# Column attention and feed-forward of a two-layer convolution and attention kernel: three column groups in work at a time, and the output tile written by ScalarE

## The chip, the cores and the metric

The kernel runs on one core of one Trainium2 chip. The metric is the time of one execution in microseconds (us), measured on the device. Five engines work side by side, each through its own queue in order: PE (TensorE, matrix products and transposes into PSUM; PEld are its weight loads), DVE (VectorE), ACT (ScalarE), POOL (GpSimd, here mostly an issuer of stores) and SP (SyncE, which issues loads).

## The reference, cut to what matters

The input is (4, 64, 256, 256) in fp32. Two layers follow each other; only the end of the second one is touched. With `h` as (batch, row, column, 64 channels) that end computes

```
hc = _ln(h.swapaxes(1, 2), cn_g, cn_b)
h = h + _lin_attn(hc, col_wq, ..., col_bo).swapaxes(1, 2)
f = _ln(h, fn_g, fn_b)
f = gelu(f @ w1.T + b1, approximate=False) @ w2.T + b2
return jnp.moveaxis(h + f, -1, 1)
```

`_ln` is a layer norm over the channels. `_lin_attn` runs along a column, over its 256 rows, with 4 heads and one value of q and k per head: q and k become elu + 1, k is divided by its sum and q by its mean over the rows, `ktv` is the sum over the rows of k times v (16 channels per head), and the output is q times `ktv`, times `wo`, plus a bias. The feed-forward goes from 64 channels to 256 and back.

## The kernel before, in words

The kernel runs in stages, one after another; intermediate results lie in HBM. The last stage, `stage_d` (L1124 to L1334), reads `hd`, the result of the row attention, and writes the output. Its unit is a *column group*: one image and 32 of its columns, with all 256 rows. There are 4 x 8 = 32 groups. A group's tile `h` has 128 partitions (rows of one half of the image) x 32 columns x 2 halves x 64 channels, 16 KB per partition, and is loaded by four DMAs on SP (L1157).

For each group there are two Python generators, which trace instructions up to a `yield` and then let the other trace:

- `attn` does the attention of the group and prepares the feed-forward. For each of eight steps `r` of 4 columns: every second step `spread` (L1160 to L1169) takes 8 columns: sum over channels (L1163, DVE), difference from the mean `xc` (L1165, DVE), its square (L1167, ACT), sum of squares (L1168, DVE). The columns are transposed (L1188, PE), copied from PSUM (`xT`, L1190, ACT) and multiplied with the weights of q and k (L1197, PE). After four steps the scores are turned back (L1201, DVE). Then comes `rstd` (L1173 a square root on ACT, L1175 a reciprocal on DVE), the scaling and bias (L1204, L1205), the exponential (`feature`, L680 and L681) and the features `f` and `kz` (L1214, L1217). With these follow the sums over the rows (L1223, L1227, L1230), the reduction to `zn` (L1234 to L1241), its transpose (L1244, L1246), the 4-head map (`mix`, L687 to L695, and L1250), and the result, added to `h` in place (L1256 and L1259 on PE, L1262 on DVE), once for each half of the rows. At last comes the norm for the feed-forward: `spread` again, `rstd`, and the normed tile `xf` of 8 columns (L1273, DVE).
- `ffn` does the feed-forward in eight turns of 4 columns: transpose of `xf` (L1283), copy `xfT` (L1285, ACT), four hidden tiles of 128x512 (L1296, PE), each with its gelu (`hg`, L1298, ACT), then the transpose of `h` into PSUM (L1304) and on top of it the second product (L1307), and the sum plus bias written to the output tile `st` (L1309, DVE). `st` holds two groups (64 columns), is written in the order row, column, so with a stride of 256 bytes, and goes to HBM with eight DMAs on POOL (L1332) after every second group.

The driver pairs `attn` of group n with `ffn` of group n-1 (`_steps`, L239: one `yield` of each in turn). So an iteration begins with the transposes of the normed tiles that the end of the iteration before has made. `h` has three buffers, `xf` five, most other tiles of the stage two or one; PSUM is shared by six tiles `mm` and two `sm`, each 128x512. The written order is a priority: the framework places instructions on each engine's queue at build time by its own estimate of when each is ready, so that the order on an engine can differ from the written one. An activation function outside of the loaded set costs ScalarE a table load (ACT_TABLE_LOAD in the trace); in this stage gelu, square root and exponential change the set.

Of the kernel before, what the change touches and what calls it, by code (L numbers as in the profile page):

```python
# [9 lines left out]
F32 = mybir.dt.float32  # L10
# [237 lines left out]
def kernel(ctx: ExitStack, tc: tile.TileContext, x, packs, fd, out, off):  # L248
# [875 lines left out]
    def stage_d():  # L1124
        with ExitStack() as cs:
# [27 lines left out]
            def load(b, g):  # L1153
                h = p.tile([128, 32, 2, C], F32, name="h", bufs=3)
                for rh in (0, 1):
                    for j in (0, 1):
                        SY.dma_start(h[:, 16 * j:16 * j + 16, rh, :], hd[b, rh * 128:(rh + 1) * 128, :, 2 * g + j, :])  # L1157
                return h

            def spread(src, n, s2):  # L1160

                s1 = p.tile([128, n], F32, tag="ln_s", name="ln_s")
                V.tensor_reduce(s1, src, AX.X, ALU.add)  # L1163
                xc = p.tile([128, n, C], F32, tag="xc", name="xc")
                V.scalar_tensor_tensor(xc, bc(s1, C), -LN_S, src, ALU.mult, ALU.add)  # L1165
                sq = p.tile([128, n, C], F32, tag="ln_sq", name="ln_sq")
                S.activation(sq, xc, AF.Square)  # L1167
                V.tensor_reduce(s2, sq, AX.X, ALU.add)  # L1168
                return xc  # L1169

            def rstd(s2, n):
                s3 = p.tile([128, n], F32, tag="ln_d", name="ln_d")
                S.activation(s3, s2, AF.Sqrt, bias=eps_t, scale=LN_S)  # L1173
                s4 = p.tile([128, n], F32, tag="ln_r", name="ln_r")
                V.reciprocal(s4, s3)  # L1175
                return s4

            def attn(h, xfs):

                qp = p1.tile([128, 32, 32], F32, name="qp")  # L1180
                v1 = p1.tile([128, 64], F32, name="v1")
                for r in range(8):
                    if r % 2 == 0:
                        k = r // 2
                        spread(h[:, 8 * k:8 * k + 8].rearrange("p c a e -> p (c a) e"), 16, v1[:, 16 * k:16 * k + 16])
# [5 lines left out]
                    yield  # L1191
                    if r % 4 == 0:
                        qk = sm()
# [5 lines left out]
                    if r % 4 == 3:  # L1199

                        V.transpose(qp[:, r // 4 * 16:r // 4 * 16 + 16].rearrange("p c m -> p (c m)"), qk)  # L1201
# [4 lines left out]
                yield  # L1206
# [8 lines left out]
                fv = f.rearrange("p r k c h -> p r k (c h)")  # L1215
                kz = p1.tile([128, 2, 128], F32, name="kz")
                V.tensor_tensor(kz.rearrange("p r (c h) -> p r c h", h=4), f[:, :, 1], rs.rearrange("p (c r) -> p r c", r=2).unsqueeze(3).to_broadcast([128, 2, 32, 4]), ALU.mult)  # L1217
                yield

                t = mm()  # L1220
                for rh in (0, 1):
                    for g in range(4):
                        T.matmul(t[g * 32:(g + 1) * 32, :], kz[:, rh, g * 32:(g + 1) * 32], h[:, 8 * g:8 * g + 8, rh, :], start=(rh == 0), stop=(rh == 1))  # L1223
                qs = sm()
# [39 lines left out]
                for hf in (0, 1):  # L1264
                    v2 = p.tile([128, 32], F32, name="v2")
                    xcs = []
                    for k in (2 * hf, 2 * hf + 1):
                        xcs.append(spread(h[:, 8 * k:8 * k + 8].rearrange("p c a e -> p (c a) e"), 16, v2[:, (k % 2) * 16:(k % 2) * 16 + 16]))
                        yield
                    rs = rstd(v2, 32)  # L1270
                    for k in (0, 1):
                        xf = p.tile([128, 8, 2, C], F32, name="xf", bufs=5)
                        V.tensor_tensor(xf.rearrange("p c a e -> p (c a) e"), xcs[k], bc(rs[:, k * 16:k * 16 + 16], C), ALU.mult)  # L1273
                        xfs.append(xf)

            def ffn(h, xfs, st, gi):


                def first(r):
                    t = mm()  # L1280
                    xf = xfs[r // 2]
                    for i in range(4):
                        T.transpose(t[:, i * 128:(i + 1) * 128], xf[:, (r % 2) * 4 + i].rearrange("p a e -> p (a e)"), ident)  # L1283
                    xT = p.tile([128, 512], F32, name="xfT")
                    S.copy(xT, t)  # L1285
                    return xT

                yield
                xT = first(0)
                for r in range(8):  # L1290
                    yield
                    hg = []
                    for i in (0, 1):
                        for rh in (0, 1):
                            t = mm()
                            T.matmul(t, w1[rh * 64:(rh + 1) * 64, i * 128:(i + 1) * 128], xT[rh * 64:(rh + 1) * 64], start=True, stop=True)  # L1296
                            g = p.tile([128, 512], F32, tag=f"hg{rh}{i}", name=f"hg{rh}{i}")
                            S.activation(g, t, AF.Gelu, bias=b1[:, i:i + 1])  # L1298
                            hg.append(g)
                    nx = first(r + 1) if r < 7 else None  # L1300
                    yield
                    y = mm()
                    for i in range(4):
                        T.matmul(y[:, i * 128:(i + 1) * 128], h[:, r * 4 + i].rearrange("p a e -> p (a e)"), ident, is_transpose=True, start=(i == 0), stop=False, skip_group_check=True)  # L1304
                    for i in (0, 1):
                        for rh in (0, 1):
                            T.matmul(y[rh * 64:(rh + 1) * 64, :], w2[:, i, :], hg[i * 2 + rh], start=False, stop=(i == 1), skip_group_check=True)  # L1307
                    c = gi * 32 + r * 4
                    V.tensor_scalar(st[:, :, c:c + 4].rearrange("p r c -> p c r"), y.rearrange("p (c r) -> p c r", c=4), K("b2"), None, ALU.add)  # L1309
                    xT = nx  # L1310

            seq = [(b, g) for b in range(B) for g in range(8)]
            hs = {0: load(*seq[0])}
            xfs = {}
            st = None
            for n in range(len(seq) + 1):
                if n + 1 < len(seq):
                    hs[n + 1] = load(*seq[n + 1])
                xfs[n] = []
                ga = attn(hs[n], xfs[n]) if n < len(seq) else None  # L1320
                gf = None
                if n >= 1:
                    b, g = seq[n - 1]
                    if g % 2 == 0:
                        st = p.tile([128, 128, 64], F32, name="st")
                    gf = ffn(hs.pop(n - 1), xfs.pop(n - 1), st, g % 2)
                _steps(ga, gf)
                if n >= 1 and g % 2 == 1:
                    for i in range(4):
                        for rh in (0, 1):  # L1330
                            r = rh * 128 + i * 32
                            G.dma_start(out[b, :, r:r + 32, g // 2 * 64:g // 2 * 64 + 64], st[rh * 64:(rh + 1) * 64, i * 32:(i + 1) * 32])  # L1332
# [22 lines left out]
```

## Time and profile before

| | |
|---|---|
| three runs | 9063.34 us median (9060.01 to 9071.98) |
| the profiled execution | 9063.4 us, span of the trace 9061.6 us |
| busy in the span | PE 8382.1 us (93%), DVE 5945.5 (66%), ACT 4740.4 (52%), POOL 1135.0 (13%) |
| first product of the last stage to its last | 6812.9 to 9033.2 us |
| last output DMA issued | 9042.3 us |
| the stage between the first and the last of the feed-forwards | 6870.5 to 8989.1 us: PE busy 1887.0, DVE 1690.6, ACT 1467.5 |

A row of the profile's groups reads: line, engine, operation, output tile <- input tiles, shape, number of instructions, then busy us in total, mean ns of one, and the engine's idle time just before them with what ended it. The chain of waits follows the work that ended last, back through whatever released each step; its lines are start, length and what. A line of the list of waits reads: who waited, for whom, us in total, times, longest. Busy PE isn't PE at its peak, since matmuls are pipelined. A fp32 product appears as two instructions, so that the four hidden tiles of a turn are eight L1296.

### The profile page before, as it was taken

How to read it: one execution, taken by the hardware profiler on the slowest of the kernel's cores; microseconds unless marked ns; L12 is line 12 of the kernel's file. 1: busy time of each engine (PE TensorE's matmuls, PEld its weight loads, DVE VectorE, ACT ScalarE, POOL GpSimd, SP SyncE). 2: the span in 40 equal slices, each digit the busy share in tenths (PEclk: the TensorE clock that was granted, in tenths of full speed). 3: DMA queues.
4: the chain of work that ended last, by engine and by line, in shares of the span. 5: the costliest groups of instructions: out<-in, count | busy, mean ns of one | idle time of the engine just before them, and what ended most of it. 6: DMA issues, size and time to landing. Idle time of an engine off the chain costs nothing. (4 is left out here: it accounts for less than half of the span.)

```text
span 9061.6 us, 136047 instructions
## 1 busy us (share of the span) xinstructions
PE 8382.1 (93%) x53934; PEld 4354.5 (48%) x53934; DVE 5945.5 (66%) x8509; ACT 4740.4 (52%) x7844; POOL 1135.0 (13%) x1828
## 2 busy tenths in 40 slices
PE   8999999789999998999999999999997888898897
PEld 7877777534444443333333344444453333333333
DVE  6666666467777775222222288888887778878876
ACT  4455555545555554222222266666655767766765
POOL 1111111112221221000000011111110000000000
PEclk9999999889999999999999999999998999999999
DMA  6677767599999998888888855555533233233232
GB/s 149 138 178 173 173 168 172 152 317 384 391 393 392 382 388 333 297 297 296 297 297 297 279 163 172 173 172 168 168 117 69 53 66 66 55 66 64 58 66 47
DMA packets 1258475, 1831.95 MB, mean 202 GB/s; under 512 B 335600, under 2 KB 1040112, under 8 KB 1196656
## 3 DMA queue, kind: packets, MB, share of 16 engines
q1 hardware_dynamic: 1053296, 1034.55, 37.8%
q0 software_dynamic: 204544, 788.69, 26.6%
q8 instruction: 428, 7.01, 0.3%
q14 instruction: 207, 1.70, 0.1%
HBM read 967.57 MB, written 788.53 MB: 194 GB/s over the span
## 5 line engine op out<-in xcount | busy, mean ns | idle before, releaser
L900 DVE TENSOR_TENSOR y<-ge,mm 128x512 f32<-128x512 f32 (+1 forms) x640 | 406.2, 635 | 1212.2 <-ACT ge L899 1212.2
L867 PE MATMUL mm<-t,w 128*128 128x512 f32 (+1 forms) x2560 | 1093.9, 566 | 19.6 <-DMA t<-td 19.6
L899 ACT ACTIVATE ge<-mm 128x512 f32<-128x512 f32 (+1 forms) x640 | 354.7, 554 | 1253.8 <-PE mm L874 1253.8
L1298 ACT ACTIVATE hg<-mm,b 128x512 f32<-128x512 f32 x1024 | 631.7, 685 | 332.6 <-PE mm L1296 330.7
L760 PE MATMUL mm<-gp,wc 128*64 128x510 f32 (+1 forms) x3072 | 702.0, 595 | 89.4 <-DVE xm L770 51.2
L867 PEld LDWEIGHTS mm<-t,w 128*128 128x128 f32 x2560 | 455.4, 190 | 648.1 <-issue 437.5
L604 PEld LDWEIGHTS mm<-wqk,gp 128*128 128x128 f32 x6144 | 711.6, 192 | 71.2 <-issue 42.4
L604 PE MATMUL mm<-wqk,gp 128*128 128x128 f32 x6144 | 733.3, 276 | 0.0
L1307 PE MATMUL mm<-hg,pack_d 128*64 128x512 f32 x2048 | 579.4, 609 | 100.7 <-ACT hg L1298 100.7
L1296 PE MATMUL mm<-xfT,w 64*128 64x512 f32 x2048 | 638.4, 666 | 4.8 <-ACT xfT L1285 4.2
L815 ACT COPY tb<-mm 128x512 f32<-128x512 f32 x512 | 300.2, 587 | 632.3 <-PE mm L809 632.0
L874 PE MATMUL mm<-t,w 64*64 64x504 f32 (+1 forms) x5120 | 575.6, 555 | 0.0
L809 PE MATMUL mm<-xl,pack_c 64*128 64x512 f32 x2048 | 511.8, 599 | 8.9 <-ACT xl L797 4.7
L760 PEld LDWEIGHTS mm<-gp,wc 128*64 128x64 f32 x3072 | 278.1, 137 | 468.0 <-issue 330.2
L314 ACT ACTIVATE ln_sq<-xn 128x1024 f32<-128x1024 f32 x256 | 274.4, 1072 | 347.1 <-DVE xn L312 347.0
L316 DVE TENSOR_REDUCE ln_v<-ln_sq 128x16 f32<-128x1024 f32 x256 | 311.9, 1219 | 147.2 <-ACT ln_sq L314 147.2
L955 PE MATMUL mm<-ya,pack_e 128*64 128x512 f32 x1024 | 381.1, 616 | 11.2 <-DMA ya<-yd 11.2
L1309 DVE TENSOR_SCALAR st<-mm,pack_d 128x512 f32<-128x512 f32 x256 | 279.1, 1090 | 169.8 <-PE mm L1307 169.8
L1167 ACT ACTIVATE ln_sq<-xc 128x1024 f32<-128x1024 f32 x256 | 266.9, 1055 | 219.9 <-DVE xc L1165 219.7
L813 DVE COPY tb<-mm 128x512 f32<-128x512 f32 x512 | 344.9, 685 | 22.3 <-PE mm L809 16.8
L1296 PEld LDWEIGHTS mm<-xfT,w 64*128 64x128 f32 x2048 | 220.9, 202 | 272.4 <-issue 159.5
L874 PEld LDWEIGHTS mm<-t,w 64*64 64x64 f32 x5120 | 158.1, 132 | 374.4 <-issue 374.4
(455 smaller groups left out, 15547.3 us busy)
## 6 DMA issues: line engine op xcount, KB each, us to landing
t<-td SPq DMA_DIRECT2D x256, 1152.0 KB, 10.5
td<-tb POOLq DMA_DIRECT2D x144, 1024.0 KB, 16.1
td<-tb POOLq DMA_DIRECT2D x288, 512.0 KB, 13.9
yd<-y POOLq DMA_DIRECT2D x128, 1152.0 KB, 10.1
ya<-yd SPq DMA_DIRECT2D x192, 512.0 KB, 5.7
xs<-in_x_dram SPq DMA_DIRECT2D x128, 512.0 KB, 6.7
projd<-pj POOLq DMA_DIRECT2D x256, 256.0 KB, 4.8
gp<-projd SPq DMA_DIRECT2D x128, 512.0 KB, 9.5
```

What stands on the lines that cost most here:

```text
L604: T.matmul(qp[:, k * 128:(k + 1) * 128], gp[:, 2 * i + k // 2, at + dx:at + dx + 128], wqk[:, dx, :], start=(dx == 0), stop=(dx == 2))
L760: T.matmul(tv[i * 64:(i + 1) * 64, :, o], wc[2 * pr + i][:, dx, :], gps[i][:, 2 * r:2 * r + 2, i_], start=(dx == 1), stop=False, skip_grou ...
L809: T.matmul(t, inT[q, hf * 128:(hf + 1) * 128], xls[b // 2, s][q, :, 2 * y:2 * y + 2].rearrange("p f y t -> p f (y t)"), start=True, stop=True)
L813: V.tensor_copy(o, i_)
L867: T.matmul(t[:, :n], w[:, 0:128], x_[:, c, :], start=True, stop=False, skip_group_check=True)
L874: T.matmul(t[po:po + 64, :n].rearrange("p (n c) -> p n c", c=64)[:, :, o], w[q:q + 64, 128:192], x_[q:q + 64, c, i_], start=False, stop=Tr ...
L899: S.activation(ge[:, :n], ts[0][k][:, :n], AF.Gelu)
L900: V.tensor_tensor(y[:, c, :].rearrange("p n c -> p (n c)"), ge[:, :n], ts[1][k][:, :n], ALU.mult)
L955: T.matmul(t[b * 64:(b + 1) * 64, :], owT, ya[:, :, 2 * r:2 * r + 2, b * 64:(b + 1) * 64].rearrange("p f y t -> p y f t"), start=True, sto ...
L1296: T.matmul(t, w1[rh * 64:(rh + 1) * 64, i * 128:(i + 1) * 128], xT[rh * 64:(rh + 1) * 64], start=True, stop=True)
L1298: S.activation(g, t, AF.Gelu, bias=b1[:, i:i + 1])
L1307: T.matmul(y[rh * 64:(rh + 1) * 64, :], w2[:, i, :], hg[i * 2 + rh], start=False, stop=(i == 1), skip_group_check=True)
```

## The change

`attn` is cut in two: `scores` (up to `f` and `kz`) and `result` (from the sums over the rows to the normed tiles). An iteration n now holds the feed-forward of group n-1, `result` of group n and `scores` of group n+1, in eight turns whose order is written out. In a turn come the hidden tiles of the next turn (`first(i + 1)`), a step of `scores` and of `result`, the second product of this turn (`second(i)`), the transpose of the turn after the next (`turn(i + 2)`), and again a step of each. So gelus are used a turn later than they are issued, and `xfT` is made at the end of the turn ahead of its use. `spread` takes two tiles of 8 columns at a time, with both sums of squares at its end. `scores` does it in turns 0 and 5, `result` in 3 and 4 (after the map in turns 0 and 1 and the additions to `h` in turn 2); `rstd` and the exponential of the scores stand together in turn 7. The output tile holds one group, is written by ScalarE (Identity with the bias `b2`, stride of 128 bytes), and is stored with four DMAs after each group, in runs of 128 bytes. `h` has four buffers and is loaded two groups ahead; `xf` has six. There are 34 iterations instead of 33. In the diff `...` stands for removed lines, which are printed above.

```diff
@@ -1151,59 +1151,86 @@
             V.memset(one, 1.0)
 
             def load(b, g):
-                h = p.tile([128, 32, 2, C], F32, name="h", bufs=3)
+                h = p.tile([128, 32, 2, C], F32, name="h", bufs=4)
                 for rh in (0, 1):
                     for j in (0, 1):
                         SY.dma_start(h[:, 16 * j:16 * j + 16, rh, :], hd[b, rh * 128:(rh + 1) * 128, :, 2 * g + j, :])
                 return h
 
-            def spread(src, n, s2):
-
-                s1 = p.tile([128, n], F32, tag="ln_s", name="ln_s")
-                V.tensor_reduce(s1, src, AX.X, ALU.add)
-                xc = p.tile([128, n, C], F32, tag="xc", name="xc")
-                V.scalar_tensor_tensor(xc, bc(s1, C), -LN_S, src, ALU.mult, ALU.add)
-                sq = p.tile([128, n, C], F32, tag="ln_sq", name="ln_sq")
-                S.activation(sq, xc, AF.Square)
-                V.tensor_reduce(s2, sq, AX.X, ALU.add)
-                return xc
-
-            def rstd(s2, n):
+            def spread(h, ks, v):
+
+                xcs, sqs = [], []
+                for k in ks:
+                    src = h[:, 8 * k:8 * k + 8].rearrange("p c a e -> p (c a) e")
+                    s1 = p.tile([128, 16], F32, tag="ln_s", name="ln_s")
+                    V.tensor_reduce(s1, src, AX.X, ALU.add)
+                    xc = p.tile([128, 16, C], F32, tag="xc", name="xc")
+                    V.scalar_tensor_tensor(xc, bc(s1, C), -LN_S, src, ALU.mult, ALU.add)
+                    sq = p.tile([128, 16, C], F32, tag="ln_sq", name="ln_sq")
+                    S.activation(sq, xc, AF.Square)
+                    xcs.append(xc)
+                    sqs.append(sq)
+                for i, k in enumerate(ks):
+                    V.tensor_reduce(v[:, 16 * i:16 * i + 16], sqs[i], AX.X, ALU.add)
+                return xcs
+
+            def rstd(v, n):
                 s3 = p.tile([128, n], F32, tag="ln_d", name="ln_d")
-                S.activation(s3, s2, AF.Sqrt, bias=eps_t, scale=LN_S)
+                S.activation(s3, v, AF.Sqrt, bias=eps_t, scale=LN_S)
                 s4 = p.tile([128, n], F32, tag="ln_r", name="ln_r")
                 V.reciprocal(s4, s3)
                 return s4
 
-            def attn(h, xfs):
-
+
+
+
+            def scores(n):
+                h = hs[n]
                 qp = p1.tile([128, 32, 32], F32, name="qp")
                 v1 = p1.tile([128, 64], F32, name="v1")
-                for r in range(8):
-                    if r % 2 == 0:
-                        k = r // 2
-                        spread(h[:, 8 * k:8 * k + 8].rearrange("p c a e -> p (c a) e"), 16, v1[:, 16 * k:16 * k + 16])
+
+                def up(r):
                     t = mm()
                     for i in range(4):
                         T.transpose(t[:, i * 128:(i + 1) * 128], h[:, r * 4 + i].rearrange("p a e -> p (a e)"), ident)
                     xT = p.tile([128, 512], F32, name="xT")
                     S.copy(xT, t)
-                    yield
-                    if r % 4 == 0:
-                        qk = sm()
+                    return xT
+
+                def score(r, xT, qk):
 
 
                     for g in range(4):
                         T.matmul(qk[g * 32:(g + 1) * 32, r % 4 * 128:r % 4 * 128 + 128], cwt, xT.rearrange("p (c n) -> p c n", c=4)[:, :, g * 32:(g + 1) * 32],
                                  start=True, stop=True)
-                    if r % 4 == 3:
-
-                        V.transpose(qp[:, r // 4 * 16:r // 4 * 16 + 16].rearrange("p c m -> p (c m)"), qk)
+
+                def back(k, qk):
+
+                    V.transpose(qp[:, k * 16:k * 16 + 16].rearrange("p c m -> p (c m)"), qk)
+
+                xT = up(0)
+                spread(h, (0, 1), v1[:, 0:32])
+                yield
+                yield
+                qk = sm()
+                for r in range(7):
+                    if r == 4:
+                        back(0, qk)
+                        qk = sm()
+                    score(r, xT, qk)
+                    xT = up(r + 1)
+                    yield
+                    if r < 5:
+                        if r == 4:
+                            spread(h, (2, 3), v1[:, 32:64])
+                        yield
+
+                score(7, xT, qk)
+                back(1, qk)
                 rs = rstd(v1, 64)
                 u = qp[:, :, 0:16].rearrange("p c (r k) -> p c r k", r=2)
                 V.tensor_tensor(u, u, bc4(rs, 2, 8), ALU.mult)
                 V.tensor_tensor(u, u, cbq.unsqueeze(1).unsqueeze(1).to_broadcast([128, 32, 2, 8]), ALU.add)
-                yield
                 e = feature(p1, u, [128, 32, 2, 8])
                 yield
                 f = p1.tile([128, 2, 2, 32, 4], F32, name="f")
@@ -1212,15 +1239,20 @@
                 for rh in (0, 1):
                     for k in (0, 1):
                         V.scalar_tensor_tensor(f[:, rh, k], uv[:, rh, :, k * 4:k * 4 + 4], 1.0, ev[:, rh, :, k * 4:k * 4 + 4], ALU.add, ALU.max)
-                fv = f.rearrange("p r k c h -> p r k (c h)")
                 kz = p1.tile([128, 2, 128], F32, name="kz")
                 V.tensor_tensor(kz.rearrange("p r (c h) -> p r c h", h=4), f[:, :, 1], rs.rearrange("p (c r) -> p r c", r=2).unsqueeze(3).to_broadcast([128, 2, 32, 4]), ALU.mult)
+                fks[n] = f, kz
+
+            def result(n):
+                h = hs[n]
+                f, kz = fks.pop(n)
                 yield
 
                 t = mm()
                 for rh in (0, 1):
                     for g in range(4):
                         T.matmul(t[g * 32:(g + 1) * 32, :], kz[:, rh, g * 32:(g + 1) * 32], h[:, 8 * g:8 * g + 8, rh, :], start=(rh == 0), stop=(rh == 1))
+                fv = f.rearrange("p r k c h -> p r k (c h)")
                 qs = sm()
                 for k in (0, 1):
                     for rh in (0, 1):
@@ -1263,73 +1295,81 @@
                     yield
                 for hf in (0, 1):
                     v2 = p.tile([128, 32], F32, name="v2")
-                    xcs = []
-                    for k in (2 * hf, 2 * hf + 1):
-                        xcs.append(spread(h[:, 8 * k:8 * k + 8].rearrange("p c a e -> p (c a) e"), 16, v2[:, (k % 2) * 16:(k % 2) * 16 + 16]))
-                        yield
+                    xcs = spread(h, (2 * hf, 2 * hf + 1), v2)
+                    yield
                     rs = rstd(v2, 32)
                     for k in (0, 1):
-                        xf = p.tile([128, 8, 2, C], F32, name="xf", bufs=5)
+                        xf = p.tile([128, 8, 2, C], F32, name="xf", bufs=6)
                         V.tensor_tensor(xf.rearrange("p c a e -> p (c a) e"), xcs[k], bc(rs[:, k * 16:k * 16 + 16], C), ALU.mult)
-                        xfs.append(xf)
...
+                        xfs[n, 2 * hf + k] = xf
+                    yield
+
+            def turn(i):
+
+                n, r = divmod(i, 8)
+                t = mm()
+                xf = xfs[n, r // 2]
+                for k in range(4):
+                    T.transpose(t[:, k * 128:(k + 1) * 128], xf[:, (r % 2) * 4 + k].rearrange("p a e -> p (a e)"), ident)
+                xT = p.tile([128, 512], F32, name="xfT")
+                S.copy(xT, t)
+                xTs[i] = xT
+
+            def first(i):
+                xT = xTs.pop(i)
+                hgs[i] = []
+                for k in (0, 1):
+                    for rh in (0, 1):
+                        t = mm()
+                        T.matmul(t, w1[rh * 64:(rh + 1) * 64, k * 128:(k + 1) * 128], xT[rh * 64:(rh + 1) * 64], start=True, stop=True)
+                        g = p.tile([128, 512], F32, tag=f"hg{rh}{k}", name=f"hg{rh}{k}")
+                        S.activation(g, t, AF.Gelu, bias=b1[:, k:k + 1])
+                        hgs[i].append(g)
+
+            def second(i):
+
+                n, r = divmod(i, 8)
+                h, hg = hs[n], hgs.pop(i)
+                if r == 0:
+                    sts[n] = p.tile([128, 128, 32], F32, name="st")
+                st = sts[n]
+                y = mm()
+                for k in range(4):
+                    T.matmul(y[:, k * 128:(k + 1) * 128], h[:, r * 4 + k].rearrange("p a e -> p (a e)"), ident, is_transpose=True, start=(k == 0), stop=False, skip_group_check=True)
+                for k in (0, 1):
+                    for rh in (0, 1):
+                        T.matmul(y[rh * 64:(rh + 1) * 64, :], w2[:, k, :], hg[k * 2 + rh], start=False, stop=(k == 1), skip_group_check=True)
+                S.activation(st[:, :, 4 * r:4 * r + 4].rearrange("p r c -> p c r"), y.rearrange("p (c r) -> p c r", c=4), AF.Identity, bias=K("b2"))
+                if r == 7:
+                    b, g = seq[n]
+                    for q in (0, 1):
+                        for rh in (0, 1):
+                            y0 = rh * 128 + q * 64
+                            G.dma_start(out[b, :, y0:y0 + 64, g * 32:g * 32 + 32], sts[n][rh * 64:(rh + 1) * 64, q * 64:(q + 1) * 64])
+                    del hs[n]
+
+            seq = [(b, g) for b in range(B) for g in range(8)]
+            N = len(seq)
+            hs, fks, xfs, xTs, hgs, sts = {}, {}, {}, {}, {}, {}
+            hs[0] = load(*seq[0])
+            for n in range(-1, N + 1):
+                if 0 <= n + 2 < N:
+                    hs[n + 2] = load(*seq[n + 2])
+                gs = scores(n + 1) if n + 1 < N else iter(())
+                gr = result(n) if 0 <= n < N else iter(())
                 for r in range(8):
...
+                    i = 8 * (n - 1) + r
+                    if 0 <= i + 1 < 8 * N:
+                        first(i + 1)
+                    next(gs, 0)
+                    next(gr, 0)
+                    if 0 <= i < 8 * N:
+                        second(i)
+                    if 0 <= i + 2 < 8 * N:
+                        turn(i + 2)
+                    next(gs, 0)
+                    next(gr, 0)
+                _steps(gs, gr)
 
     stage_d()
 
```

## The prediction

> **What bounds the kernel now.** I read the slices of the span first (the last quarter, from 6812 us, is the stage that is changed), then the chain of waits to find its period: the first L1296 of a group comes at 7485.50 and again at 7553.78 us, so one group takes 68.28 us. There are 32 of them: from 6870.5 to 8989.1 us are 31 periods, and 31 x 68.3 = 2117. Then I cut one period into four stretches (columns: us; busy us of PE, PEld, DVE, ACT, POOL, each with its instructions; granted clock; DMA share; GB/s):
>
> ```profile
> 7485.50:7502.50 17.00, 17.00 (x94) 7.62 (x98) 15.85 (x16) 16.14 (x24) 0.00 (x0) 0.91 0.00 1
> 7502.50:7519.40 16.90, 15.07 (x86) 6.19 (x82) 13.60 (x19) 14.67 (x20) 0.00 (x0) 1.00 0.00 0
> 7519.40:7537.40 18.00, 17.96 (x110) 7.95 (x111) 8.75 (x17) 8.88 (x16) 0.10 (x1) 1.00 0.01 1
> 7537.40:7553.80 16.40, 10.81 (x66) 4.89 (x66) 16.33 (x18) 7.64 (x12) 2.48 (x3) 0.98 0.61 138
> ```
>
> The limit changes: PE in the first and third stretch, nobody quite in the second, DVE in the fourth, where the attention of the next group ends with its norm while PE waits. The chain of waits (start us, us, what) tells how that ends:
>
> ```profile
> 7548.80 1.13 DVE v L1168
> 7549.93 0.98 DVE st L1309
> 7550.91 0.18 DVE ln_r L1175
> ...
> 7551.12 1.24 DVE xf L1273
> ...
> 7552.40 0.67 PE mm L1283 x4
> ...
> 7553.14 0.59 ACT xfT L1285
> ```
>
> PE's new group cannot begin before xf, and the list of waits over eight periods has the bill: 26.5 us, 3.3 in each period.
>
> ```profile
> PE mm L1283 <- DVE xf L1273: 26.5, 8, 3.3
> ```
>
> After that wait the eight L1296 take 3.42 us where others take 1.92, and the granted clock of that stretch is 0.91: 1.5 us more. The Trainium skill (TensorE: Matmul & The Clock Gate, Part 1) says that one idle window of about 3.4 us halves the clock; the 3.32 us wait and the doubled spacing behind it agree nearly, and the 1.5 us is taken from the trace.
>
> PE's work without waits, summed from the chain's steps: one feed-forward turn is L1296 1.92, L1283 0.59, L1304 0.44, L1307 1.87, together 4.82; the last group, which runs alone, repeats every 4.81 us (9004.45, 9009.25, 9014.07). Eight are 38.6; 8 x (L1188 0.59 + L1197 0.36) = 7.6; L1223, L1227, L1230 3.2; L1244 and L687 0.7; twice L1256 and L1259 3.9. Sum 54.0 of 68.3: 14.3 us per group are waits. ACT is busy 47.3 and DVE 54.5.
>
> **The change, part by part.** (1) *Order.* An iteration now holds the feed-forward of group n-1, `result` of n and `scores` of n+1. Its instructions on PE are the old ones, but xf of a group is written in turns 3 and 4 and first wanted in turn 6 (`turn(i + 2)`), and L1307 uses hidden tiles a whole turn old. So the 3.3 us, the 1.5 us behind it and the waits of L1307 for the gelus (25.4 us in eight periods on PE's row, 3.2 each) can go: 8.0 us. What is late next is ACT, as follows.
>
> (2) *The output add.* DVE loses eight of the first row below, 8.7 us of its 54.5. ACT gets eight Identity activations with a bias from PSUM, written with a stride of 128 bytes, which the trace of before does not have. From below: the same form written densely. From above: L797, Identity with scattered writes, half the size, doubled: 1.62.
>
> ```profile
> L1309 DVE TENSOR_SCALAR st<-mm,pack_d 128x512 f32<-128x512 f32 x256 | 279.1, 1090 | 169.8 <-PE mm L1307 169.8
> L549 ACT ACTIVATE pj<-mm,bin__121 128x512 f32<-128x512 f32 x256 | 174.2, 682 | 83.3 <-PE mm L547 77.0
> L797 ACT ACTIVATE xl<-mm,pack_c 128x256 f32<-128x256 f32 x512 | 333.5, 811 | 0.8 <-PE mm L795 0.8
> L1298 ACT ACT_TABLE_LOAD x126 | 161.7, 1283 | 2.3
> L1173 ACT ACT_TABLE_LOAD x96 | 123.2, 1283 | 1.8
> L681 ACT ACT_TABLE_LOAD x95 | 121.9, 1283 | 1.7
> ```
>
> I take 1.15 us, nearest to the strided write itself: DVE pays 1090 against 684 for a dense 128x512 (L1262), 0.41 more; 0.68 + 0.41 = 1.09, and L797's slope without the fixed part, about 1.8 ns per element, gives 1.19. Eight are 9.2 us. No Identity row (L549, L797, L1043) has a table load, so it adds none.
>
> (3) *Tables.* A group has eight loads now: in these eight periods L1298 32, L1173 24, L681 8. After, a sqrt in turns 3, 4 and 7, and the exp straight behind the last: seven, 1.28 less. If gelus are put between sqrt and exp it stays eight. ACT's total: 47.3 - 1.3 + 9.2 = 55.2, more than PE's 54.0.
>
> (4) *Loads and stores.* `load` moves one group ahead with a fourth buffer, four issues on SP as before; their landing (5.4 us) has a period of cover. The store becomes four DMAs per group instead of eight per two, as many issues on POOL (1.10 each), which nothing else there waits for. Runs are 128 bytes instead of 256, so twice as many; the DMA share of the stage is 0.28. Even doubled it hides. At the end the last burst has 16384 runs as before with half the bytes: between 14 and 28 us of tail; I keep the measured 28.
>
> **The sum by turns.** Work is spread unevenly over the eight turns, so engines' totals are not enough. PE: 8.6, 6.5, 9.6, then 5.8, 5.8, 5.8, 6.7, 5.2 (4.82 plus its share of the attention). ACT: each turn 4.2 (gelus 2.42, xfT 0.59, st 1.15); xT 0.53 in turns 0 to 5, two in 6; Squares 2.0 in 0, 3, 4, 5; qT 0.4 in 0; two table loads and a sqrt, 2.9, in 3 and 4; 4.8 in 7 (sqrt, exp, three loads). So 7.1, 4.7, 4.7, then 9.6, 9.6, 6.7, 5.3, 9.0. DVE: 9.4, 2.4, 5.1, then 10, 10, 8, 0, 4.5. Turns 0 to 2 are PE's: 24.7 against ACT's 16.5. Turns 3 to 7 are ACT's: 40.2 against DVE's 32.5 and PE's 29.3. Together 64.9. Against that: ACT may lag by about a turn (two buffers of the hidden tiles and of xfT) and catch up in turns 0 to 2, up to 4.2 gained. For it: the exp waits for four DVE operations of 2.4 us, less its own load 1.1; and ACT's order will be wrong somewhere, as at 7541 to 7543 us now, where gelus stood some 2.1 us behind a Square whose xc was late. 64.9 - 4.2 + 1.1 + 2.1 = 63.9; I take **64.0** per group.
>
> One rule of the Trainium skill speaks against the change: ScalarE: Activation LUTs, Rules for kernel authors, wants adds on VectorE. By it the add stays on DVE: ACT's five turns fall by 5 x 1.15 to 34.4, DVE's rise by 5 x 1.09 to 38.0, and the period would be 62.7 instead of 64.9, so the rule may be right here by about 2 us a group. The same page, What ACT_TABLE_LOAD costs, puts a switch at 2.66 us with a drain of 1.38; the trace has a gelu ending at 7510.67, the load, and the sqrt beginning at 7511.98, 1.31 in all, so by the page's price the period would be some 7 us longer, and I go by the row.
>
> *Outside the periods.* Scores of the first group end at 6839 us as now. The iteration with result 0 and scores 1 has 49.5 us of DVE work, taken as 51: 6890. Then 30 full periods, one without scores (22.3 of PE, then ACT's 31) 53, the last feed-forward 8 x 4.81 - 1.9 + 1.2 = 38, the tail 28. Span = 7009 + 30 x period; the profiled run took 9063.4 with a span of 9061.6, so 1.8 more: 7011 + 30 x 64.0 = **8931 us**. That run stands at the median of the three (9063.3). Equal time needs a period of 68.4.
>
> **Rivals.** *Evener* (0.21): the lag does its work without wrong orders, 64.9 - 4.2 = 60.7 or less, 8832 us. For it: PE and ACT have both almost nothing else to wait for. Against: both would be over 90% busy, and no stretch of a period above has two engines that full at once but the first.
>
> *Xf's wait returns each turn, as xfT's* (0.20, slower). xfT is the last of ACT's turn, behind st, which waits for L1307, and the next L1296 needs it at once: PE stands 0.1 + 1.15 + 0.1 + 0.59 - 0.59 (the L1283 meanwhile) = 1.35 us in turns without other work for it, and ACT then stands 1.25 us until the first gelu (as L1296 at 7525.11 and its gelu at 7526.27). One in turns 0 to 2 and five in 3 to 7: 64.9 + 1.35 + 6.2 = 72.5, 9186 us. It decides from 68.4, that is when over half of those 7.6 us come true. For it: `first` follows `turn` with nothing between in turns 3, 4 and 7. Against: the order on an engine isn't the written one (L1197 stands between L1296s at 7495.5), and while xfT is copied the next L1307s have their inputs.
>
> *It moves waits and no time* (0.09): half of that comes true, period 68.3, 9060 us. Also with a dear st (1.62) and a part of it.
>
> **The numbers.** The forecast (periods 62 to 67) has 0.50. Faster: it, the even case, and a little of the third, 0.73; within 0.2% (18 us, about what a measurement of this kernel can tell from no change) 0.07; slower 0.20. The range reaches to a period of 59.3 below, which leaves out 0.07, and to 70.0 above, which leaves out 0.11: 8790 to 9111.
>
> **What would show it.** Right: no L1283 that waits 3 us for xf; DVE near 46 us a period; st on ACT at 1.1 to 1.2 us; seven table loads; ACT full in the part with the sqrts, PE full in the part with L1223 and L1259. Wrong: PE waiting for xfT in most turns (the second rival), or st far from 1.15, each 0.1 us of which is worth 5 x 0.1 x 30 = 15 us; and if DVE still ends the chain in the second half, the turns' sum named the wrong engine.

## The result, and the profile after

The changed kernel takes 9338.2 us (median of four runs, 9335.4 to 9342.9) against 9064.6 of the kernel before (four runs): ratio 1.030, 95% interval [1.028, 1.032]. It is 273.6 us slower; the forecast was 8931, the range 8790 to 9111. One of the rivals, at 9186, named the wait that is found below. One execution among all that follow, of the last version in the table, took 12521 us at a granted clock of 0.64 (0.98 in the others) and isn't counted.

The period, 68.28 us before, is 77.1 now (25 periods from 7128.89 to 9057.24 us; single ones take 75.9 to 78.1). Two stretches of one period first, turns 0 to 2 and turns 3 to 7, cut at the first product of each (columns as in the prediction: us; busy us of PE, PEld, DVE, ACT, POOL; granted clock; DMA share; GB/s):

```profile
7514.28:7541.16 26.88, 26.59 (x161) 11.75 (x160) 7.37 (x17) 15.08 (x23) 4.40 (x4) 0.94 0.54 112
7541.16:7591.36 50.20, 36.27 (x196) 15.32 (x192) 39.66 (x44) 41.01 (x55) 2.49 (x2) 0.89 0.12 27
```

The forecast had 24.7 us of PE and 40.2 of ACT here. ACT's 41.0 are there, but the turns take 50.2: the engine that should be full stands for 9.2 us of them. The list of waits over some eight periods (7504.1 to 8118.7 us) says for whom (who waited, for whom, us in all, times, longest):

```profile
PE mm L1324 <- ACT xfT L1315: 73.2, 40, 2.9
ACT hg L1326 <- PE mm L1324: 69.7, 55, 2.2
ACT st L1342 <- PE mm L1341: 60.1, 30, 3.5
```

The line of xf (3.3 us a period before) is gone, as meant. In its place PE waits 9.2 us a period for the copy xfT, in five turns of eight, and ACT waits 8.7 us for those products, L1324. They wait for each other in turn, as the chain of waits shows (start us, us, what):

```profile
7550.50 1.12 ACT st L1342
7551.62 0.43 ACT xfT L1315
7552.06 0.04 issue
7552.10 1.76 PE mm L1324 x4
...
7557.48 1.84 ACT hg L1326 x3
...
7559.80 0.34 ACT st L1342
...
7561.60 1.07 ACT ln_sq L1170
7562.67 0.48 ACT xfT L1315
7563.15 0.04 issue
7563.20 2.13 PE mm L1324 x4
```

L1324 is `first`, L1315 the copy in `turn`, L1341 and L1342 are `second`. The turns from 7552.10 to 7581.66 go once around each: copy, products, gelus, st, Square, copy. They are not the whole part: before them the chain runs over VectorE's passes for the norm (7541.27 to 7549.52), behind them over ScalarE alone to the next period. The last feed-forward runs alone and has a shorter loop, without squares and roots: copy, products, then PE's second product (L1341) in place of the gelus, st, copy. Three lines of PE and ACT there, a turn apart (start us, us, engine, what, idle before and what ended it):

```profile
9269.27 1.99 PE L1324 MATMUL mm<-xfT,w 64*128 64x512 f32 x8 [1.06 <-ACT xfT L1315]
...
9270.43 2.42 ACT L1326 ACTIVATE hg<-mm,b 128x512 f32<-128x512 f32 x4 [1.21 <-PE mm L1324]
...
9275.36 1.99 PE L1324 MATMUL mm<-xfT,w 64*128 64x512 f32 x8 [1.06 <-ACT xfT L1315]
```

A turn is 6.09 us, where the same instructions took 4.81 before. That is 1.28 for the place of the copy and of the add, with both engines idle in it.

The second part of the loss is PE's speed. The products of the hidden tiles, over the same eight periods:

```profile
L1324 PE MATMUL mm<-xfT,w 64*128 64x512 f32 x512 | 178.6, 796 | 78.9 <-ACT xfT L1315 73.2 <-DVE h L1294 5.6
```

Their mean was 668 ns in eight periods before. It is a mixture: eight products take 1.99 us, or, behind some of the waits, up to 3.8. Before, slow ones came at one place in each period, now on average at four (98 places in 25 periods; 536 of 1600 products take over 1 us, before 137 of 1586), and the granted clock of a period is 0.89 instead of 0.97.

### The profile page after: what moved, and what is told of

The parts are those of the page before. It is cut to its first block, busy times and chain, and to the rows that moved or that the text cites. A ratio compares the mean times of both kernels' runs of the same rounds, so it can differ in the third digit from the quotient of the medians.

```text
span 9338.5 us, 136286 instructions
## 1 busy us (share of the span) xinstructions
PE 8457.3 (91%) x53934; PEld 4378.5 (47%) x53934; DVE 5697.6 (61%) x8253; ACT 5005.1 (54%) x8100; POOL 1203.8 (13%) x1828
## 5 line engine op out<-in xcount | busy, mean ns | idle before, releaser
L1324 PE MATMUL mm<-xfT,w 64*128 64x512 f32 x2048 | 705.2, 787 | 320.5 <-ACT xfT L1315 298.6
L1341 PE MATMUL mm<-hg,pack_d 128*64 128x512 f32 x2048 | 500.3, 609 | 0.0
L1324 PEld LDWEIGHTS mm<-xfT,w 64*128 64x128 f32 x2048 | 220.4, 223 | 583.8 <-ACT xfT L1315 342.3
L1348 POOL DMA_DIRECT2D out_dram<-st x128 | 208.8, 1635 | 2081.8 <-ACT st L1342 1944.6
L1342 ACT ACTIVATE st<-mm,pack_d 128x512 f32<-128x512 f32 x256 | 293.5, 1146 | 237.9 <-PE mm L1341 237.9
```

What stands on the lines that cost most here:

```text
L1324: T.matmul(t, w1[rh * 64:(rh + 1) * 64, k * 128:(k + 1) * 128], xT[rh * 64:(rh + 1) * 64], start=True, stop=True)
L1341: T.matmul(y[rh * 64:(rh + 1) * 64, :], w2[:, k, :], hg[k * 2 + rh], start=False, stop=(k == 1), skip_group_check=True)
L1342: S.activation(st[:, :, 4 * r:4 * r + 4].rearrange("p r c -> p c r"), y.rearrange("p (c r) -> p c r", c=4), AF.Identity, bias=K("b2"))
```

## The experiments

*Theory A:* the copy xfT at the turn's end, wanted at once, closes a loop in which ScalarE's whole work of a turn stands, and PE's slower clock lengthens it. *Theory B:* it is ScalarE's load alone (the add). *Theory C:* it is that squares, roots and table loads now stand in blocks. "Copy early" below means that `turn(i + 2)` stands straight behind `first(i + 1)`.

| version | us | ratio to before, 95% interval |
|---|---|---|
| as changed | 9338.2 | 1.030 [1.028, 1.032] |
| add on VectorE | 8994.7 | 0.992 [0.991, 0.994] |
| copy early | 9054.7 | 0.999 [0.998, 1.000] |
| both | 8896.3 | 0.982 [0.980, 0.983] |
| both, add on ScalarE in turns 3 to 5 | 8952.7 | 0.988 [0.986, 0.990] |
| both, scores' second passes in turn 1 | 8951.3 | 0.988 [0.986, 0.989] |
| the last, add on ScalarE in turns 0 to 2 | 8949.8 | 0.988 [0.986, 0.989] |
| as changed, PE's waits filled | 9192.7 | 1.014 [1.013, 1.016] |
| as changed, copy on VectorE | 9193.6 | 1.015 [1.013, 1.017] |
| as changed, add written densely | 9229.7 | 1.019 [1.016, 1.021] |
| as changed, squares for roots | 9171.2 | 1.012 [1.010, 1.014] |
| before, add on ScalarE | 9127.9 | 1.007 [1.006, 1.009] |
| before, PE's wait filled | 9057.1 | 0.999 [0.998, 1.000] |

**The two halves, alone and together.** The add back on VectorE:

```diff
-                S.activation(st[:, :, 4 * r:4 * r + 4]..., y..., AF.Identity, bias=K("b2"))
+                V.tensor_scalar(st[:, :, 4 * r:4 * r + 4]..., y..., K("b2"), None, ALU.add)
```

> The changed kernel with the output add back on VectorE, everything else as changed. Its period is 76.8 us; PE waits 9.2 us of it for xfT and the first products behind those waits run at half speed (some 7 us). Theory A (xfT is copied at the end of the turn and wanted at once): the copy loses st ahead of it, 1.15 us in some five turns of eight, but keeps its place, so the period falls by 3 to 7 us, 9130 to 9250 us. Theory B (the added load on ScalarE is the cause): with ScalarE back at 45 us a period the loss is gone, 9060 us or less. Theory C (blocks of squares, roots and table loads on ScalarE in turns 3 to 7): hardly a change, 9280 us or more.

The copy early:

```diff
                         first(i + 1)
+                    if 0 <= i + 2 < 8 * N:
+                        turn(i + 2)
                     next(gs, 0)
                     next(gr, 0)
                     if 0 <= i < 8 * N:
                         second(i)
-                    if 0 <= i + 2 < 8 * N:
-                        turn(i + 2)
```

> The changed kernel with the transpose and copy of the turn after the next written straight behind the hidden tiles (first, turn, steps, second, steps), so that the copy has the second product to hide behind; the add stays on ScalarE. Theory A: the waits of PE for xfT and the slowed products behind them go, the period is 62 to 66 us, 8870 to 8990 us, faster than before. Theories B and C: ScalarE has the same work in the same blocks, the period stays at 72 to 77 us, 9190 to 9340 us.

The first gained 343 us, which was B's number and far over A's; the second 284, less than A wanted and more than B and C allowed. So neither theory as written. What told them apart was both at once:

> The changed kernel with both: output add on VectorE and the transpose and copy of the turn after the next straight behind the hidden tiles. Alone the first gave 8994.7 us (period 65.6), the second 9054.7 (67.9). Theory A (a loop from the copy xfT over the products to the gelus, as long as ScalarE's work of a turn plus 1.25 us): with both, nothing of the loop is left and the parts of the period count, 24.7 us of PE and 38 of VectorE, 62.7: 8890 us (8860 to 8960). Theory B (ScalarE's load alone, the place of the copy is worth nothing once the load is gone): as with the add on VectorE alone, 8975 to 9015 us.

8896.3 us: A's number. With the add on VectorE the copy's place is still worth 98 us, with the add on ScalarE 284; the add is worth 343 with the late copy, 158 with the early one. The two are not a sum: with the late copy, the add also lengthens the loop that the copy closes. What changed besides, the loads two groups ahead and the smaller output tile with runs of 128 bytes, is the same in the version with both, so the loss isn't theirs.

The 158 us that remain are not the loop's as A has it. With the copy early and the add on ScalarE the two stretches are:

```profile
7502.72:7531.35 28.63, 27.01 (x161) 11.90 (x161) 11.50 (x23) 19.98 (x28) 6.62 (x5) 0.94 0.65 133
7531.35:7570.81 39.46, 32.07 (x192) 13.67 (x188) 35.75 (x37) 35.34 (x50) 0.00 (x0) 1.00 0.05 11
```

The second is as long as the sum had said (40.2), but the first takes 28.6 us instead of 24.7: from 7539.73 the chain of waits runs over ScalarE, but for 3.0 us on VectorE (from 7567.16), past the end of turn 7, to the exponential at 7573.97 and a gelu that ends at 7576.61. By this chain ScalarE's load is most of the limit there, and B has its part. In the version with both, the two stretches are:

```profile
7526.53:7552.81 26.28, 25.32 (x162) 11.66 (x162) 17.81 (x30) 15.70 (x24) 6.62 (x5) 1.00 0.69 134
7552.81:7589.43 36.62, 31.21 (x193) 13.36 (x189) 36.50 (x39) 31.71 (x46) 0.00 (x0) 1.00 0.09 21
```

PE fills the first to 96%, VectorE the second wholly (36.50 of 36.62), and the clock is full: 62.9 us in all. The engines' sums, 24.7 and 38.0, hold here to 0.2 us together; singly they miss by 1.6 and 1.4, which cancel. The copy's wait isn't gone with the early copy. Over 1840 us it is, first with the add on ScalarE (27 periods), then with both (29):

```profile
PE mm L1324 <- ACT xfT L1315: 130.4, 100, 2.7
PE mm L1324 <- ACT xfT L1315: 116.4, 59, 2.2
```

That is 4.8 and 4.0 us a period instead of 9.2. With both, it stands in the stretch that VectorE fills, and costs nothing that shows.

**The add alone, in the old order.** The same exchange in the kernel before, the other way round.

> The kernel before with one part of the change alone: the output add on ScalarE (stride 256 bytes). Theory A: the copy xfT stays early, so little happens; VectorE's last stretch loses two adds (2.2 us), the stretch with the roots gains about as much on ScalarE: 9000 to 9130 us. Theory B: ScalarE goes to 56 us a period and bounds it: 9200 us or more. Theory C: as A.

64 us slower, the upper end of A's span. There the copy has the second product to hide behind, and ScalarE's 9 us more cost 2.1 a period. B is out as the whole cause.

**What stands in the loop costs time.** Three runs changed one part each. The dense add:

```diff
+                S.activation(st.rearrange("p r c -> p (r c)")[:, 512 * r:512 * r + 512], y, AF.Identity, bias=K("b2"))
```

> The changed kernel with ScalarE's output add written densely, 512 elements in a row; the values of the output then stand in another order. The add should fall from 1.15 us to about 0.68. Theory A: 0.47 us off ScalarE's part of the loop in five to eight turns, 2.4 to 3.8 us a period, and a little of the slowed products: 9210 to 9270 us. If only the order on the queue counts: 9320 us or more.

The add fell from 1148 to 690 ns, the period by 108.5 / 30 = 3.6 us, which is eight times the difference, with the order on PE, ScalarE and VectorE unchanged. It need not be every turn's add: the mean of L1324 fell too, from 792 to 749 ns, so a part of the 3.6 is PE's clock. The roots:

```diff
-                S.activation(s3, v, AF.Sqrt, bias=eps_t, scale=LN_S)
+                S.activation(s3, v, AF.Square, bias=eps_t, scale=LN_S)
```

> The changed kernel with a square in place of the square root, so that the normed values are others and no table is loaded for the roots: two loads and their place behind late sums of squares go in turns 3 and 4 each, one in turn 7, 6.4 us of ScalarE a period. Theory A (ScalarE's work of a turn stands in the loop in full): 5 to 8 us a period with what the clock gives back, 9100 to 9190 us. If the table loads lie beside other waits: 9280 us or more.

167 us, 5.6 a period: as A said, but less than what was taken away. Six table loads of 1283 ns went (two a period are left of eight), 7.7 us. C is right in this, that the table loads count while the loop stands, but they were there before too. And the copy on another engine:

```diff
                 xT = p.tile([128, 512], F32, name="xfT")
-                S.copy(xT, t)
+                V.tensor_copy(xT, t)
```

> The changed kernel with the copy xfT on VectorE instead of ScalarE, in its place at the end of the turn; the output add stays on ScalarE. ScalarE loses 4.9 us a period, VectorE gets 8 x 0.69. Theory A: the copy is no longer behind squares, roots and st, so the loop is cut: period 65 to 69 us, 8960 to 9080 us, unless VectorE's passes of 1.2 us stand ahead of it, up to five in turns 3 to 5, which would give the wait back: then 9200 us or more. Theory B: about half of what the add's move gave (4.9 of 9.2 us), 9150 to 9180 us.

9193.6, about what was named if VectorE's passes stand ahead of the copy. The list of waits (1800 us, 25 periods) has the wait under its new name, 10.8 us a period:

```profile
PE mm L1324 <- DVE xfT L1315: 270.1, 100, 4.2
```

A ScalarE that is lighter by the copy gains 145 us, not the 284 of the copy in its early place: on the other engine the copy is late again.

**PE's clock.** The waits were filled with work of no use:

```diff
+                ts = [mm() for k in range(4)]
+                if i % 8 in (0, 1, 5, 6, 7):
+                    for t in ts:
+                        for k in range(3):
+                            T.transpose(t[:, k * 128:(k + 1) * 128], ident, ident)
...
-                        t = mm()
+                        t = ts[k * 2 + rh]
```

> The changed kernel with twelve extra transposes of the identity (1.76 us of PE at full speed) ahead of the hidden tiles of five turns in eight, those whose first products wait for xfT now; they write PSUM that the products then overwrite, so nothing of the result changes. If the products behind a wait are slow because PE had stood idle, they return from 3.4 to 1.92 us, some 7 us a period: 9110 to 9250 us though PE has more to do. If they are slow for another reason (their operands or PSUM slots), the time stays or grows: 9330 to 9420 us.

145.5 us faster, though PE has 60 transposes more in each period. The products' mean (L1329 here) falls to 631 ns, only 40 of 1600 take over 1 us, and the clock of a period is 0.98:

```profile
L1329 PE MATMUL mm<-xfT,w 64*128 64x512 f32 x1792 | 488.0, 631 | 149.3 <-ACT xfT L1315 129.5 <-DVE h L1294 19.8
7487.00:7559.40 72.40, 65.04 (x409) 31.45 (x409) 46.51 (x60) 55.45 (x77) 6.62 (x5) 0.98 0.29 59
```

That the products were slow because PE had stood is shown by this. What it cost is less sure. The gain is 4.9 us a period, over half of the difference to the kernel before; the transposes take PE's time, so the clock may have cost more, but they also moved other instructions (the transposes L1195 of turn 5 came at 7566.57 behind the products of 7563.20, now they come at 7516.76 ahead of those of 7518.81), and how much that gained was not tried. The same in the kernel before, with twenty transposes ahead of the first transposes of each feed-forward:

> The kernel before, unchanged but for twenty extra transposes of the identity (2.9 us of PE at full speed) ahead of the first transposes of each feed-forward, where PE stands 3.3 us for xf; they write PSUM that is then overwritten. If the 1.5 us that the first eight products lose there comes from PE having stood idle, they return from 3.42 to 1.92 us and 31 periods save up to 46 us: 9015 to 9045 us, with more work. If not, nothing is saved and what does not fit in the wait is added: 9063 to 9110 us.

No change that can be told (9057.1; 0.9993 [0.998, 1.000]). In 11 of the 30 groups from 6937.27 to 8917.26 us the products are slow all the same, so both kinds stand side by side, with the same work: in every group the twenty transposes stand from 6.4 to 3.4 us ahead of the first product, and behind them PE waits 0.73 and 0.67 us. From the chain of waits, the starts of four groups (L1299 is the product of the hidden tiles):

```profile
7142.76 1.99 PE mm L1299 x8
...
7210.78 1.99 PE mm L1299 x8
...
7346.82 3.52 PE mm L1299 x8
...
7415.43 1.99 PE mm L1299 x8
```

A group with a fast start lasts 68.02 us (7142.76 to 7210.78), one with a slow start 68.61 (7346.82 to 7415.43). The slow products are 1.5 us longer and cost 0.6 (up to 0.8 in other groups). A group of before took 68.28 with slow products, so the extra transposes cost some 0.3 themselves.

**Three attempts at more.** The add by turns, and the scores' second passes (two means, two differences, two squares) in turn 1:

```diff
+                o, i_ = st[:, :, 4 * r:4 * r + 4]..., y...
+                if r in (3, 4, 5):
+                    S.activation(o, i_, AF.Identity, bias=K("b2"))
+                else:
+                    V.tensor_scalar(o, i_, K("b2"), None, ALU.add)
```

> As the version with both, but the output add on ScalarE in turns 3, 4 and 5, where VectorE has 10, 10 and 8 us of work, and on VectorE in the others. If the parts of a period can't lend each other time, it is 24.7 (PE, turns 0 to 2) + 28 (VectorE, 3 to 5) + 12 (ScalarE, 6 and 7) = 64.7 against 24.7 + 31.3 + 12 = 68.0 with all adds on VectorE, so up to 100 us faster than that version. If they can, or if the add on ScalarE stands ahead of a copy that PE needs, it is equal or slower by up to 60 us.

```diff
                     if r < 5:
-                        if r == 4:
+                        if r == 0:
                             spread(h, (2, 3), v1[:, 32:64])
```

> The version with both (8896.3 us, period 62.9), and the second pair of mean and square passes of the scores in turn 1 instead of turn 5. By the sums VectorE's 38 us of turns 3 to 7 become 30.7, so that ScalarE's 32.4 end there, and turns 0 to 2 have 26.3 us of VectorE's: 58.7, 8770 us (8750 to 8850). If the map and the additions to h, which wait in VectorE's queue behind these passes, hold PE up in turns 1 and 2: 8880 to 8960 us.

> As the version with the passes in turn 1, but the output add on ScalarE in turns 0 to 2, where it has 13 us of work otherwise. By the sums VectorE's 26.3 us become 23.0 and PE's 24.7 end there: 57.1, 1.6 us a period less than that version, some 50 us. If the add on ScalarE stands ahead of what PE needs next, as in the mixed version, it is slower than that version by 30 to 60 us.

All three are 54 to 56 us slower than the version with both. The first should have gained up to 100 us if the parts of a period can't lend each other time, so they do. An add ahead of the copy was the other reason named for a loss, but PE's wait for xfT is no longer than with both (3.7 us a period against 4.0), and what the 56 us are stays open. In the second the sums failed: turns 3 to 7 did shrink, to 34.6 us (first products at 7506.12 and 7540.75), but the next turn 0 took 13.1 (to 7553.85). Its chain:

```profile
7541.01 1.13 DVE ln_s L1166
7542.14 0.62 DVE qp L1209
7542.76 1.12 DVE xc L1168
...
7549.51 0.69 DVE f L1241 x3
...
7551.32 0.26 DVE kz L1243
...
7551.63 1.92 PE mm L1254 x16
```

Passes now stand between the steps to the features in VectorE's queue, and L1254, which needs kz, is late. That this is all of the 55 us was not tried. The third added nothing to the second, so ScalarE's slack in turns 0 to 2 was worth nothing there.

## Why the prediction was wrong

- *That xf's wait goes:* right; no line of it is left. *The slow products behind it, 1.5 us:* they were put down at their full length; the fill of the wait before shows 0.6 to 0.8 for a group, and here they came back at four places in a period instead of one.
- *The sizes:* right. st 1148 ns (1.15), ScalarE 41.0 us in turns 3 to 7 (40.2), VectorE 45.5 a period (46). Three things were not. There are eight table loads a period, not seven, since gelus came between root and exponential, which was named. The 7 us estimated there by the price of a switch (the Trainium skill, ScalarE: Activation LUTs, What ACT_TABLE_LOAD costs) are 9.5 by the figures beside it, seven times 2.66 - 1.31. VectorE's turns were added up to 49.4 us where the text itself names 46, and in turns 3 to 7 it works 39.7 us, not 32.5. And 1.19 us for the add doesn't come out of L797's row (811 ns less 256 x 1.8 leave 350, and with 512 x 1.8 that is 1.27), so that the middle, 1.15, fits to 2 ns is partly luck.
- *The step that failed:* that PE and ScalarE overlap in turns 3 to 7, so that this part is ScalarE's 40.2 us, and that "ACT may lag by about a turn ... up to 4.2 gained", that is 64.9 - 4.2 + 1.1 + 2.1. A lag needs work that may wait; the copy may not, because the products follow it on PE with nothing between. ScalarE stood 9.2 us in the part where it was to be full. The 40.2 became 50.2, the 24.7 became 26.9, and nothing was gained by a lag: 77.1 for the 64.0.
- *The argument that carried it:* against the second rival it was said that the order on an engine isn't the written one and that, while xfT is copied, the next second products have their inputs. They had: at 7548.4 us the last gelu for the next L1341 was done, and PE stood from 7549.3 to 7552.1. But PE's queue had L1324 first; L1338 came at 7556.15. Why the framework left it so when it set the order, no trace can show. An order seen once to differ from the written one was taken as a promise that it would.
- *The rival's price:* 1.35 us for the wait in a turn without other work; in the last feed-forward PE waits 1.06 and the turn is 1.28 longer. It gave 72.5 for the period; measured 77.1. It had nothing for PE's clock, which is up to about that much (4.9 us a period with the waits filled), and nothing for squares and roots in the loop; the split wasn't measured.
- *The rule that spoke against the change* (the Trainium skill, ScalarE: Activation LUTs, Rules for kernel authors: adds on VectorE) was given 62.7 us for the period by the sums; the version that follows it, with the copy early, has 62.9. The traces' reason is the place in ScalarE's queue and ScalarE's load, not the add's own time (1148 ns there, 1101 on VectorE). Without the copy early it has some 66.
- *The turns themselves* are what the forecast took them for: three groups in work at a time, with the add on VectorE and the copy early, run 1.8% faster than the kernel before, 8896 us. That the forecast's 8931 lies near is chance: there VectorE is the limit in turns 3 to 7, not ScalarE. Add and place lost 442.

## What to carry to other kernels

Before adding up engines by stretch, follow each value from its writer to its next reader in the written order; where a copy is issued last on one engine and read first on the next, the turn can be as long as the loop, and instructions ahead of the copy hold up both engines. Write such a copy as soon as its source is there, so that other products of PE cover it, and keep late work (an output add) off its queue; here the add there still cost 158 us with the copy early. Don't count on the framework to reorder it.

## What the runs showed of the hardware

PE lost its full clock after shorter waits than the 3.32 us of before. After 2.34 us (7504.10) the eight products took 3.22 us, after 2.92 us (7563.20) 3.44, and after 1.07 us that followed another of 1.20 (7572.81) 3.65. But the length alone doesn't decide. With a single wait of 1.06 us in each turn of 6.09 us, as in the last feed-forward, they stayed at 1.99, and with the copy early they stayed at 1.99 behind a wait of 2.70 us (7547.60). The Trainium skill (TensorE: Matmul & The Clock Gate, Part 1) speaks of an idle window of about 3.4 us; here 2.34 us were enough in one place and 2.70 were not in another, and the measurement decides.

When a wait falls seems to matter too. The clock moves in steps of 3.41 us: in one period of the changed kernel it is 0.50 from 7504.72, 7514.96, 7552.51, 7562.75 and 7572.99, which lie whole multiples of 3.41 us apart. Two steps as changed, then two with the copy early (columns as above):

```profile
7501.31:7504.72 3.41, 1.07 (x8) 0.60 (x8) 2.89 (x4) 3.41 (x6) 0.00 (x0) 1.00 0.00 0
7504.72:7508.13 3.41, 3.41 (x18) 1.02 (x15) 1.38 (x2) 3.38 (x5) 0.00 (x0) 0.50 0.00 0
7543.35:7546.76 3.41, 1.55 (x8) 0.29 (x4) 2.23 (x4) 3.37 (x5) 0.00 (x0) 1.00 0.00 0
7546.76:7550.17 3.41, 2.57 (x16) 1.17 (x20) 3.41 (x4) 3.41 (x6) 0.00 (x0) 1.00 0.00 0
```

The wait of 2.34 us lies in one step, that of 2.70 us across two. In the kernel before with its wait filled, the same waits of 0.73 and 0.67 us had slow products behind them in 11 of 30 groups. That the place in the step decides is a reading of these rows and was not tested.

ScalarE's write with a stride of 128 bytes cost 1148 ns for 128x512 where the dense one cost 690; VectorE paid 1101 for the same pattern, and had paid 1090 for a stride of 256 bytes.
